# Attention and selective scan in one kernel: gates in the convolutions' banks, and new places for denominators, sums and statistics

## The chip, the core and the metric

The kernel runs on one core of a Trainium2 chip. The core has a matrix engine (TensorE, PE in the profile), a vector engine (VectorE, DVE), an activation engine (ScalarE, ACT), a general engine (GpSimd, POOL) and a sequencer that here only issues transfers (SyncE, SP). Each takes its instructions in the order in which the program issues them and waits on semaphores for the others. Matrix products are written to PSUM, which the kernel uses in banks of 128 partitions by 512 numbers. The metric is the device time in microseconds (us), the median over runs.

## The reference, cut to what matters

```python
x = x + attention(_gn(x), Wq, bq, Wkv, bkv)   # x: (8, 512, 48, 48); _gn: 32 groups of 16 channels
x = x + multiscale_mamba(_gn(x), ...)         # four blocks of 128 channels

# attention: 8 heads of 64, causal and linear, L = 2304 tokens
Q, K, V = elu(q) + 1, elu(k) + 1, v
den = 1 / (einsum('nhld,nhld->nhl', Q, cumsum(K)) + 1e-10)
S = S + k[..., :, None] * v[..., None, :];  o = einsum('nhk,nhkv->nhv', q, S)    # per token
out = o * den

# mamba, for block i of 4 (its input is block i plus the result of block i-1)
xp, z = split(u @ Wi.T)                       # 256 + 256 channels
xs = silu(causal_conv4(xp) + bc)
dt, Bm, Cm = split(xs @ Wx.T)                 # 8, 16, 16
delta = softplus(dt @ Wdt.T + bdt)
h = exp(delta * A) * h + (delta * xs) * Bm    # per token; 256 channels x 16 states
y = (sum_n(h * Cm) + xs * D) * silu(z)
xm = y @ Wo.T                                 # then fused with the input by a maximum and two sigmoids of means
```

Everything is float32.

## The kernel before, in words

The tokens of a sample are cut into six chunks of LC = 384. The Mamba part runs as 192 jobs, one for each sample, block of channels and chunk. Two streams take alternate samples, so that jobs of two samples interleave. A job consists of eight slots, a slot of four scans (`scan`, L830, 128x385 on DVE). Half slots are numbered through the whole program; a job has 16 of them, and this document counts them from 0 in each job.

For each scan ACT computes the factor exp(delta*A), called a decay (`decay`, L819), into a PSUM bank, and DVE reads it from there. In each slot DVE further computes one product for the next slot (`product`, L809), and POOL the last columns of that product (L798) and the weighting by C (L846). PE sums the weighted states (`gather`, L853) into `yp`. After four slots, half of the channels, `yp` is multiplied by the gate (`gated`, L865). When both halves are done, the output's projection (`project`, L871) and the maximum (L882) follow as a task called `finale`.

Six PSUM banks rotate. `take` hands out a free one, to decays and to all other work alike; a bank comes back at the place in the program where `free` is called, and whoever takes it next waits by semaphore until its last reader is done. `ahead(n)` issues decays as long as fewer than n are outstanding and a bank is free; n is 3 in the slots and 5 just before the two batches of activations named next.

Everything else is issued between the scans by tasks: generators that stop at a `yield` with a due time and the number of banks that they want. "1" means one half slot after the task's last step, a pair (h, gap) means at half slot h, and at least gap after the last step. `beside` is called in each half slot and steps the tasks that are due and whose banks are free. Each engine's order follows from this plan alone.

The tasks that matter here:

- `Job.prepare` prepares a job some ten slots before its first scan: the convolution as four products per half (`conv`, L635), the gates' products (`gate`, L646), a batch of four Silus on ACT (L670 to L675) with a load of the activation table before it and one after it, the projection to dt, B and C (L681, L686), the steps (L694) and a batch of two Softplus (L705), again between two table loads. In the steady state the Silu batch stands in half slot 14 and the Softplus batch in half slot 2 of the 16 that follow.
- `chunk` is the attention for one chunk, at half slots given by `times[m]`, usually half slot 3 of a job plus the number in `at(j)`: projections of q, k and v (L288), the feature map on ACT (L300, L301) and its end on DVE (L345, L353), the running sums of k (`kc`, L364), the product pr (L374), transposes of k and v (L381) and their copies kl and v (L385, L386), the denominators `den` and the state sums `ds` in one bank called `both` (L393, L398), the reciprocal and the additions to the state S (L401 to L410), the spread of the reciprocals over the rows (`rdb`, L414, and transposes `rb`, L418), and then scores and outputs (L423 to L454).
- `statistics` computes the group norm's statistics of a sample (`bn_stats`, L242, from pieces that `piece` loads, L248), `group_norm` the norm from them, and from those of the attention's result.
- `Stream.pass_on` moves a stream to its next block, and carries each chunk over with up to three activations (L596, L597, L601), which in the steady state stand in half slot 2.

Of the kernel before, what the change touches and what calls it, by code (L numbers as in the profile page):

```python
# [9 lines left out]
F32 = mybir.dt.float32  # L10
# [6 lines left out]
P = 128  # L17
# [32 lines left out]
def attention_then_mamba_kernel(  # L50
# [110 lines left out]

    def group_norm(stats, n, name, bufs):


        bank = Banks()
        yield "1", 1
        mv = small.tile([P, n, 2], F32, tag=f"mv{n}", name=f"mv_{name}", bufs=1)
        for ct in range(n):
            nc.vector.bn_aggr(mv[:, ct, :], stats[:, ct].rearrange("p c s -> p (c s)"))
        mean_ps = bank()  # L170
        nc.tensor.matmul(mean_ps[:, 0:n], grp, mv[:, :, 0], start=True, stop=True)
        yield "1", 0
        gm = small.tile([P, 3, n], F32, tag=f"gm{n}", name=f"gm_{name}", bufs=1)
        nc.vector.tensor_copy(gm[:, 0, :], mean_ps[:, 0:n])
        nc.vector.tensor_sub(gm[:, 1, :], mv[:, :, 0], mean_ps[:, 0:n])
        bank.free()
        if n == 1:
            nc.vector.tensor_scalar(
                gm[:, 2, :], gm[:, 1, :], gm[:, 1, :], mv[:, 0, 1:2], ALU.mult, ALU.add
            )  # L180
        else:
            nc.vector.tensor_mul(gm[:, 2, :], gm[:, 1, :], gm[:, 1, :])
            nc.vector.tensor_add(gm[:, 2, :], gm[:, 2, :], mv[:, :, 1])
        yield "0", 1
        var_ps = bank()
        nc.tensor.matmul(var_ps[:, 0:n], grp, gm[:, 2, :], start=True, stop=True)
        yield "1", 0
        nc.vector.tensor_scalar_add(gm[:, 2, :], var_ps[:, 0:n], 1e-5)
        bank.free()
        norm = small.tile([P, 3, n], F32, tag=f"norm{n}", name=f"norm_{name}", bufs=bufs)  # L190
        nc.gpsimd.tensor_tensor(norm[:, 0, :], gm[:, 2, :], power[:, 0:n], ALU.pow)
        yield "1", 0
        for i, factor in ((0, -1.0), (1, float(L))):
            for ct in range(n):
                nc.vector.tensor_scalar(
                    norm[:, 1 + i, ct : ct + 1],
                    gm[:, i, ct : ct + 1],
                    norm[:, 0, ct : ct + 1],
                    factor,
                    ALU.mult,  # L200
                    ALU.mult,
                )
        return norm
# [5 lines left out]
    def statistics(b):  # L209

        xv = x[b].rearrange("(t p) l -> p t l", p=P)
        stats = small.tile([P, 4, NC, 6], F32, tag="stats_a", name=f"stats_a{b}", bufs=1)
        if b == 0:
# [19 lines left out]
        else:  # L233
            for ct in range(4):
                for c in range(NC):
                    yield "2", 0
                    if (ct, c) == (0, 0):
                        nxt = piece(b, 0)
                    xs = nxt
                    i = ct * NC + c + 1  # L240
                    nxt = piece(b, i) if i < 4 * NC else None
                    nc.vector.bn_stats(stats[:, ct, c, :], xs)  # L242
        norms[b] = yield from group_norm(stats, 4, f"a{b}", 2)
# [24 lines left out]
    def chunk(m):  # L268
# [10 lines left out]
        def at(j, gap=1):  # L279
            return times[m] + j, gap  # L280
# [61 lines left out]
        ex = feature(qp, qb)  # L342
        yield at(2), 0
        q = new("q", 2)
        nc.vector.scalar_tensor_tensor(q, ex, 1.0, qp, ALU.min, ALU.add)  # L345
        bank.free()
        yield at(2, 0), 1
        kp, kb = project(1)
        yield at(3), 0
        ex = feature(kp, kb)  # L350
        yield at(4), 0
        k = new("k", 2)
        nc.vector.scalar_tensor_tensor(k, ex, 1.0, kp, ALU.min, ALU.add)  # L353
# [14 lines left out]
        if ksum is not None:  # L368
            kept = new("kept")
            nc.scalar.copy(kept[64:128], kc[64:128])  # L370
            save(ksum[:, cols], kept[64:128])
# [16 lines left out]

        yield at(12), 1
        both = bank()  # L390
# [5 lines left out]
        for i in range(more):  # L396
            for h in heads_of:
                nc.tensor.matmul(ds[h, i, :], kl[:, i, h], v[:, i, h], start=True, stop=True)  # L398
        yield at(14), 0
        rd = small.tile([P, 2 * NT], F32, tag="rd", name=f"rd_{n}", bufs=1)  # L400
# [5 lines left out]
        for i in range(more):  # L406
            if c == 0 and i == 0:
                nc.vector.tensor_copy(S[:, place[1], :], ds[:, 0, :])
            else:
                nc.vector.tensor_add(S[:, place[i + 1], :], S[:, place[i], :], ds[:, i, :])  # L410
        bank.free()
        yield at(15), 0
        rdb = new("rdb", 1, (P, 2 * NT, 64))
        nc.scalar.copy(rdb, rd.unsqueeze(2).to_broadcast([P, 2 * NT, 64]))  # L414
        yield at(16), 1
        rb = bank()[:, 0:LC].rearrange("p (i t) -> p i t", i=NT)
        for i in range(NT):
            nc.tensor.transpose(  # L418
                rb[:, i, :], rdb[:, 2 * i : 2 * i + 2, :].rearrange("p e d -> p (e d)"), ident
            )  # L420
        yield at(18), 0

# [33 lines left out]
        if c + 1 == NC:  # L456
            norm = yield from group_norm(stats, 1, f"m{b}_{o}", 8)
            flush()
            done[b, o] = norm
# [156 lines left out]
    class Job:  # L616
# [6 lines left out]
        def prepare(self):  # L623
# [19 lines left out]

            def gate(h):
                zp = bank()[:, 0:LC]
                nc.tensor.matmul(  # L646
                    zp,
                    wi[:, 256 + h * P : 256 + (h + 1) * P],
                    xi[:, c0 + 3 : c0 + 3 + LC],
                    start=True,  # L650
                    stop=True,
                )
                return zp

# [3 lines left out]
            converting.append(n)  # L658
            yield "1", 1
            xc0 = conv(0)  # L660
            yield "2", 2
            xc1 = conv(1)
            zp0 = gate(0)
            yield "1", 0
            xs = self.xs = mpool.tile([P, 2, LC], F32, tag="xs", name=f"xs_{n}")
# [4 lines left out]
            nc.scalar.activation(xs[:, 0, :], xc0, AF.Silu, bias=pv[:, 0:1])  # L670
            bank.free()
            zp1 = gate(1)
            nc.scalar.activation(xs[:, 1, :], xc1, AF.Silu, bias=pv[:, 1:2])
            nc.scalar.activation(sz[0], zp0, AF.Silu)
            nc.scalar.activation(sz[1], zp1, AF.Silu)  # L675
            converting.clear()
            bank.free(3, late=True)
            yield "1", 1
# [65 lines left out]
            for h in range(2):  # L744
                yield "1", 0
                nc.gpsimd.tensor_tensor(delta[:, h, :], delta[:, h, :], xs[:, h, :], ALU.mult)  # L746
            first = 2 * self.start
            yield "2", 0
# [208 lines left out]
    def finale(job):  # L957
        yield "0", 1
        job.project()
        yield "1", 0  # L960
        job.maximum()
        if job.c == NC - 1:
            yield from job.stream.pass_on()

    begun, put, counted = 0, 0, list(range(1, B))

    def begin(latest):

        nonlocal begun, put
        while counted and times[parts.index((counted[0], 0, 0))] - 64 <= half_no[0]:  # L970
            tasks.append(Task(statistics(counted.pop(0))))
# [52 lines left out]
    def at(k):  # L1024
        return jobs[k // SLOTS], k % SLOTS
# [166 lines left out]
```

## Time and profile before

| | |
|---|---|
| Median of 3 runs | 9329.64 us (9327.21 to 9330.81) |
| The profiled execution | 9323.3 us, of which 9321.5 us are the span from its first to its last instruction |
| Mean granted TensorE clock | 0.948 |
| First scan starts, last scan ends | 222.5 us, 9273.6 us |
| DVE idle between them | 785 us |
| Scans (L830) | 6144, mean 938 ns |
| Decays (L819) | 6144, mean 579 ns |
| Table loads on ACT | 768, 1283 ns each |

The profile shows one execution. A busy share counts an engine's instructions in the span; since neighbours overlap by some 0.08 us, this document also uses the time from the start of an instruction to the start of the next. A row of the wait view names who waited and for whom, then the total in us, the number of waits and the longest. A row of the timeline gives the start, the time it took, engine, line, operation, the tile written and those read, and the number of instructions that it merges; in brackets stands the idle time of the engine before it, and what ended it.

### The profile page before, as it was taken

The numbers are of one execution on the slowest core, as the hardware profiler recorded it, in microseconds if no ns is written. First come the engines' busy times: TensorE is split into PE (matmuls) and PEld (weight loads), VectorE is DVE, ScalarE is ACT, GpSimd is POOL, SyncE is SP. The second block draws the span as 40 slices with busy tenths as digits, with TensorE's granted clock in tenths as the row PEclk, the third lists the DMA queues.
The fourth block names the chain that finished last, engine by engine and source line by source line (L and its number), as shares of the span: only waits on it lengthen the run. The fifth ranks groups of instructions, "written<-read, shape, count | busy, mean of one in ns | idle before, by whom it ended". The sixth has DMA issues, their size and how long they took to land.

```text
span 9321.5 us, 120629 instructions
## 1 busy us (share of the span) xinstructions
PE 7735.1 (83%) x35714; PEld 3673.0 (39%) x35714; DVE 8348.4 (90%) x11640; ACT 6580.2 (71%) x12656; POOL 8080.8 (87%) x5635
## 2 busy tenths in 40 slices
PE   7888888888888888888888888888888888888865
PEld 4444444433344444443343444443333434444321
DVE  3899999999999999999999999999999999999997
ACT  3677777777777777777777777776777777777775
POOL 2788888889988898889998888888998888888998
PEclk9999999999999999999999999999999999999977
DMA  6566666667666666666766666667666666666654
GB/s 189 158 169 173 175 174 168 180 189 198 188 169 176 177 179 172 176 183 189 196 182 178 174 175 173 174 170 194 192 184 182 176 176 172 173 171 175 167 153 129
DMA packets 1002899, 1642.84 MB, mean 176 GB/s; under 512 B 138592, under 2 KB 797312, under 8 KB 1002240
## 3 DMA queue, kind: packets, MB, share of 16 engines
q1 hardware_dynamic: 1002240, 1635.13, 64.1%
q8 instruction: 283, 4.64, 0.2%
q14 instruction: 376, 3.08, 0.1%
HBM read 1309.06 MB, written 325.58 MB: 175 GB/s over the span
## 4 chain that ended last, share of the span: by engine, by line
DVE 39%; ACT 20%; PE 18%; issue 7%; DMA 7%; POOL 6%; SPq 2%; DVEq 0%; POOLq 0%; ACTq 0%
DVE u L830 23%; DVE u L809 8%; PE bank L288 7%; ACT bank L819 6%; PE bank L635 4%; POOL u L846 4%; ACT L819 3%; PE yp L853 3%; PE bank L646 2%; ACT L705 2%; DMA B<-scr 2%; DMA C<-scr 1%; ACT bank L301 1%; ACT delta L705 1%; DVE sm L436 1%
## 5 line engine op out<-in xcount | busy, mean ns | idle before, releaser
L830 DVE TENSOR_TENSOR_SCAN u<-bank,u 128x385 f32<-128x385 f32 (+1 forms) x6144 | 5475.1, 938 | 530.5 <-ACT bank L819 503.2
L846 POOL TENSOR_TENSOR u<-u,C 128x1536 f32<-128x1536 f32 x1536 | 4885.1, 3180 | 219.5 <-DVE u L830 112.6
L819 ACT ACTIVATE bank<-dr,av 128x385 f32<-128x385 f32 (+1 forms) x6144 | 3431.3, 579 | 1556.9 <-DVE u L830 1113.3
L853 PE MATMUL yp<-u,cst 128*64 128x384 f32 x12288 | 2429.9, 514 | 282.7 <-ACT yp L787 146.3
L798 POOL TENSOR_TENSOR u<-B,dxr 128x512 f32<-128x512 f32 x1536 | 1959.9, 1276 | 22.4 <-DMA dxr<-xscr 19.0
L288 PE MATMUL bank<-xn,wq_sb 128*128 128x384 f32 x4608 | 1855.1, 552 | 48.8 <-DVE u L830 31.7
L809 DVE TENSOR_TENSOR u<-B,dxp 128x1024 f32<-128x1024 f32 x1536 | 1834.7, 1195 | 10.7 <-ACT dxp L782 10.7
L853 PEld LDWEIGHTS yp<-u,cst 128*64 128x64 f32 x12288 | 788.3, 139 | 1476.6 <-issue 903.5
L635 PE MATMUL bank<-xi,wk 128*128 128x384 f32 x3072 | 1118.2, 507 | 280.1 <-ACT kl L385 172.7
L288 PEld LDWEIGHTS bank<-xn,wq_sb 128*128 128x128 f32 x4608 | 929.1, 212 | 862.9 <-issue 215.1
L635 PEld LDWEIGHTS bank<-xi,wk 128*128 128x128 f32 x3072 | 563.7, 193 | 862.2 <-ACT kl L385 254.1
L844 POOL COPY state<-u 128x4 f32<-128x4 f32 x1280 | 243.8, 190 | 740.6 <-DVE u L830 738.0
L300 ACT ACTIVATE ex<-bank,bqkv_sb 128x384 f32<-128x384 f32 x384 | 221.3, 576 | 561.6 <-PE bank L288 539.2
L787 ACT ACTIVATE yp<-xs,pv 128x384 f32<-128x384 f32 x384 | 223.4, 582 | 405.7 <-DVE yz L865 405.7
L819 ACT ACT_TABLE_LOAD x382 | 490.1, 1283 | 6.7
L746 POOL TENSOR_TENSOR delta<-delta,xs 128x384 f32<-128x384 f32 x384 | 385.8, 1005 | 95.5 <-DMA dscr<-delta 84.3
L418 PE MATMUL bank<-cst,rdb 128*128 128x128 f32 x576 | 112.7, 310 | 426.1 <-DVE u L830 334.7
L694 PE MATMUL bank<-dbc,wd 9*128 9x384 f32 x768 | 316.3, 524 | 65.1 <-ACT dbc L686 29.0
L646 PE MATMUL bank<-xi,wi 128*128 128x384 f32 x768 | 297.8, 500 | 59.8 <-ACT xs L670 59.8
L871 PE MATMUL bank<-yz,wo 128*128 128x384 f32 x768 | 297.6, 509 | 34.1 <-DVE yz L865 19.4
L449 PE MATMUL bank<-sm,v 128*64 128x128 f32 x2304 | 257.2, 301 | 42.4 <-DVE u L830 40.6
L418 PEld LDWEIGHTS bank<-cst,rdb 128*128 128x128 f32 x576 | 66.8, 153 | 558.9 <-ACT xb L601 272.5
(109 smaller groups left out, 7860.3 us busy)
## 6 DMA issues: line engine op xcount, KB each, us to landing
B<-scr SPq DMA_DIRECT2D x1536, 192.0 KB
C<-scr SPq DMA_DIRECT2D x1536, 192.0 KB
xn<-xn SPq DMA_DIRECT2D x192, 768.0 KB
dr<-dscr SPq DMA_DIRECT2D x768, 192.0 KB
dxr<-xscr SPq DMA_DIRECT2D x768, 192.0 KB
dscr<-delta SPq DMA_DIRECT2D x192, 384.0 KB
xscr<-delta SPq DMA_DIRECT2D x192, 384.0 KB
xn<-in_x SPq DMA_DIRECT2D x48, 768.0 KB
```

The costliest lines, as they stand in the source:

```text
L288: nc.tensor.matmul(ps, wq_sb[:, kt, j * 512 + o * P : j * 512 + (o + 1) * P], xn[:, kt, :], start=(kt == 0), stop=(kt == 3),)
L635: nc.tensor.matmul(xc, wk[:, k, h * P : (h + 1) * P], xi[:, c0 + k : c0 + k + LC], start=(k == 0), stop=(k == 3),)
L646: nc.tensor.matmul(zp, wi[:, 256 + h * P : 256 + (h + 1) * P], xi[:, c0 + 3 : c0 + 3 + LC], start=True, stop=True,)
L694: nc.tensor.matmul(vp, wd[32:41, h * P : (h + 1) * P], dbc[32:41, :], start=True, stop=True)
L746: nc.gpsimd.tensor_tensor(delta[:, h, :], delta[:, h, :], xs[:, h, :], ALU.mult)
L798: nc.gpsimd.tensor_tensor(u[:, :, :, 1 + LC - TAIL :], self.B[s % 4][:, :, cols].unsqueeze(2).to_broadcast(shape), self.dxr[s // 4][:, :, ...
L809: nc.vector.tensor_mul(u[:, :, :, 1 : 1 + LC - TAIL], self.B[s % 4][:, :, cols].unsqueeze(2).to_broadcast(shape), self.dxp.unsqueeze(1).to ...
L819: nc.scalar.activation(dA[:, cols], self.dr[h][:, g, cols], AF.Exp, scale=self.w[6][:, 2 * h + g, q + j : q + j + 1],)
L830: nc.vector.tensor_tensor_scan(u[:, j, g, cols], dA[:, cols], u[:, j, g, cols], 0.0, ALU.mult, ALU.add,)
L846: nc.gpsimd.tensor_tensor(h, h, self.C[s % 4].unsqueeze(2).to_broadcast([P, NG, 2, LC]), ALU.mult)
L853: nc.tensor.matmul(self.yp[g * 64 : g * 64 + 64, 0:LC], pair_sum, u[:, j, g, 1:], start=False, stop=(s % 4 == 3 and j == NG - 1), skip_gro ...
L871: nc.tensor.matmul(self.xm[:, 0:LC], self.w[2][:, h, :], self.yz[:, h, :], start=(h == 0), stop=(h == 1),)
```

## The change

The gates' products no longer take banks of their own: `gate(h, zp)` writes into the bank of the convolution once the Silu has read it. The steps of `prepare` up to there get fixed half slots. `den` and `ds` are computed two half slots earlier, and what follows from them as well; the transposes `rb` go into the bank `both` instead of a new one, so that it is held until q has been multiplied. The projection of k no longer comes after q's end, and q's end moves one half slot back. `kept` uses the buffer of `before`. The statistics of samples 2 to 7 are spread to one piece in 16 half slots, from two buffers, and the steps of `group_norm` get places of their own. `finale` asks for "1" instead of "0".

```diff
-    def group_norm(stats, n, name, bufs):
+    def group_norm(stats, n, name, bufs, places=("1", "1", "0", "1", "1")):
...
-            for ct in range(4):
-                for c in range(NC):
-                    yield "2", 0
-                    if (ct, c) == (0, 0):
-                        nxt = piece(b, 0)
-                    xs = nxt
-                    i = ct * NC + c + 1
-                    nxt = piece(b, i) if i < 4 * NC else None
-                    nc.vector.bn_stats(stats[:, ct, c, :], xs)
+            when = begins[b] + b % 2
+            for i in range(4 * NC):
+                yield (when - 2, 1) if b > 1 else "1", 0
+                xs = piece(b, i)
+                yield (when, 1) if b > 1 else "1", 0
+                nc.vector.bn_stats(stats[:, i // NC, i % NC, :], xs)
+                when += PERIOD
...
-        yield at(2), 0
-        q = new("q", 2)
+        yield at(2), 1
+        kp, kb = project(1)
+        yield at(3), 0
+        q, k = new("q", 2), new("k", 2)
         nc.vector.scalar_tensor_tensor(q, ex, 1.0, qp, ALU.min, ALU.add)
         bank.free()
-        yield at(2, 0), 1
-        kp, kb = project(1)
-        yield at(3), 0
         ex = feature(kp, kb)
         yield at(4), 0
-        k = new("k", 2)
...
-            kept = new("kept")
+            kept = new("before")
...
-        yield at(12), 1
+        yield at(10, 0), 1
         both = bank()
...
-        yield at(14), 0
+        yield at(12), 0
         rd = small.tile([P, 2 * NT], F32, tag="rd", name=f"rd_{n}", bufs=1)
...
-        bank.free()
-        yield at(15), 0
+        yield at(13), 0
         rdb = new("rdb", 1, (P, 2 * NT, 64))
         nc.scalar.copy(rdb, rd.unsqueeze(2).to_broadcast([P, 2 * NT, 64]))
-        yield at(16), 1
-        rb = bank()[:, 0:LC].rearrange("p (i t) -> p i t", i=NT)
+        yield at(14), 0
+
+        rb = both[:, 0:LC].rearrange("p (i t) -> p i t", i=NT)
...
-        yield at(18), 0
+        yield at(16), 0
 
         nc.vector.tensor_mul(q, q, rb.rearrange("p i t -> p (i t)"))
         bank.free()
...
-            norm = yield from group_norm(stats, 1, f"m{b}_{o}", 8)
+            norm = yield from group_norm(
+                stats, 1, f"m{b}_{o}", 8, [(times[m] + j, 1) for j in (28, 29, 29, 30, 31)]
+            )
...
-            def gate(h):
-                zp = bank()[:, 0:LC]
+            def gate(h, zp):
...
-            yield "1", 1
+            first = 2 * self.start
+            yield (first - 21, 0), 1
             xc0 = conv(0)
-            yield "2", 2
+            yield (first - 19, 2), 1
             xc1 = conv(1)
-            zp0 = gate(0)
-            yield "1", 0
+            yield (first - 18, 1), 0
...
             nc.scalar.activation(xs[:, 0, :], xc0, AF.Silu, bias=pv[:, 0:1])
-            bank.free()
-            zp1 = gate(1)
+
+            gate(0, xc0)
             nc.scalar.activation(xs[:, 1, :], xc1, AF.Silu, bias=pv[:, 1:2])
-            nc.scalar.activation(sz[0], zp0, AF.Silu)
-            nc.scalar.activation(sz[1], zp1, AF.Silu)
+            gate(1, xc1)
+            nc.scalar.activation(sz[0], xc0, AF.Silu)
+            nc.scalar.activation(sz[1], xc1, AF.Silu)
             converting.clear()
-            bank.free(3, late=True)
+            bank.free(2, late=True)
...
     def finale(job):
-        yield "0", 1
+        yield "1", 1
         job.project()
...
+    begins = {}
+    for b in counted:
+        first = times[parts.index((b, 0, 0))]
+        begins[b] = (first - 20) // PERIOD * PERIOD - 4 * NC * PERIOD - 2 if b > 1 else first - 64
...
-        while counted and times[parts.index((counted[0], 0, 0))] - 64 <= half_no[0]:
+        while counted and begins[counted[0]] - 4 <= half_no[0]:
             tasks.append(Task(statistics(counted.pop(0))))
```

## The prediction

> **What bounds the kernel now.** First the head of the page: VectorE (DVE) is the busiest engine.
>
> ```profile
> PE 7735.1 (83%) x35714; PEld 3673.0 (39%) x35714; DVE 8348.4 (90%) x11640; ACT 6580.2 (71%) x12656; POOL 8080.8 (87%) x5635
> ```
>
> The first scan starts at 222.5 us, the last ends at 9273.6; DVE is idle for 785 us between. Second, the waits of DVE in that stretch (who waited for whom: us in total, times, longest):
>
> ```profile
> DVE u L830 <- ACT bank L819: 503.2, 194, 4.7
> DVE q L345 <- ACT bank L301: 108.1, 54, 4.2
> DVE k L353 <- ACT bank L301: 56.6, 136, 1.0
> DVE gm_m L188 <- PE bank L186: 29.4, 31, 1.1
> ```
>
> A scan that waits for its decay is most of it: about once in each of the 192 jobs. Third, the timeline of one job's end on DVE, ACT and PE (start, us, engine, line):
>
> ```profile
> 4247.63 1.19 DVE L809 TENSOR_TENSOR u<-B,dxp 128x1024 f32<-128x1024 f32 x1
> 4248.74 2.65 DVE L830 TENSOR_TENSOR_SCAN u<-bank,u 128x385 f32<-128x385 f32 x3
> 4254.33 0.96 DVE L830 TENSOR_TENSOR_SCAN u<-bank,u 128x385 f32<-128x385 f32 x1 [2.94 <-ACT bank L819]
> ```
>
> ```profile
> 4247.91 1.10 ACT L819 ACTIVATE bank<-dr,av 128x385 f32<-128x385 f32 x2
> 4249.03 1.28 ACT L670 ACT_TABLE_LOAD   x1
> ...
> 4251.91 0.49 ACT L675 ACTIVATE sz<-bank 128x384 f32<-128x384 f32 x1
> 4252.42 1.28 ACT L819 ACT_TABLE_LOAD   x1
> 4253.71 1.09 ACT L819 ACTIVATE bank<-dr,av 128x385 f32<-128x385 f32 x2
> ```
>
> ```profile
> 4247.69 2.85 PE L635 MATMUL bank<-xi,wk 128*128 128x384 f32 x8 [1.29 <-ACT kl L385]
> 4250.38 1.49 PE L646 MATMUL bank<-xi,wi 128*128 128x384 f32 x4
> ```
>
> ACT leaves the decays for a batch of four Silus between two table loads. Three decays are ready; DVE uses them up and waits 2.94 us. The softplus batch has the same shape, and four decays ready:
>
> ```profile
> 4260.39 1.20 DVE L809 TENSOR_TENSOR u<-B,dxp 128x1024 f32<-128x1024 f32 x1
> 4261.50 3.50 DVE L830 TENSOR_TENSOR_SCAN u<-bank,u 128x385 f32<-128x385 f32 x4
> 4264.92 1.20 DVE L809 TENSOR_TENSOR u<-B,dxp 128x1024 f32<-128x1024 f32 x1
> 4266.03 0.55 DVE L865 TENSOR_TENSOR yz<-yp,sz 128x384 f32<-128x384 f32 x1
> 4266.94 1.81 DVE L830 TENSOR_TENSOR_SCAN u<-bank,u 128x385 f32<-128x385 f32 x2 [0.36 <-issue]
> ```
>
> ```profile
> 4262.78 1.28 ACT L705 ACT_TABLE_LOAD   x1
> 4264.08 0.87 ACT L705 ACTIVATE delta<-bank 128x384 f32<-128x384 f32 x2
> 4264.97 1.28 ACT L819 ACT_TABLE_LOAD   x1
> 4266.26 0.59 ACT L819 ACTIVATE bank<-dr,av 128x385 f32<-128x385 f32 x1
> ```
>
> Four scans, the product and yz just last until the next decay ends at 4266.85: no wait for ACT, and nothing to spare.
>
> **What the Trainium skill says.** "ScalarE: Activation LUTs", What ACT_TABLE_LOAD costs: about 1283 ns for the load plus about 1380 ns of drain. The load agrees (1283 ns in the rows); the drain does not show: the next activation starts 1.29 us after the load's start, and I use that. "PSUM — Partial Sum Buffer", Engine vs sequencer instructions: ACT's queue is strictly first in, first out, and matmuls run in program order. The trace agrees (the gates L646 start as the convolution's eight L635 end), so a static order decides what can hide. "Perfetto Trace Analysis", Identifying the Most-Contended Engine: a bubble that repeats can mean too few buffers. Here it is one per job, and the buffers are the six PSUM banks.
>
> **The change, part by part.** I use durations from start to start of neighbours, as the timelines give them: scan 0.86, product L809 1.11, other 384-wide DVE operations 0.45 to 0.47, decay 0.52, table load 1.29. A job is 8 slots, 16 half slots. All counts come from the order in which both programs' instructions stand on each engine.
>
> (1) Silu batch, ACT's side. Gates now write the banks of the two convolutions, so each waits for its Silu; and den and ds (L393, L398), moved two half slots up, now stand on PE between the second convolution and the gates, in 173 of 190 jobs. Their own runs took 0.83 and 0.57 us, 1.40 together. Before, gate 0 starts 1.35 us after the table load's start and sz at 2.24; after, gate 0 at 2.75, gate 1 0.64 later, its end (0.85 on) at 4.25, the last Silu at 4.28 instead of 2.88. The next decay is 1.40 us later. Were PE not delayed, the wait for the Silus alone would cost about 0.6 (xs ends at 1.87, a gate takes 0.80); that is the low end, 1.8 the high one if den waits for more.
>
> (2) Silu batch, DVE's side. Decays ready: before 6 banks less xc0, xc1 and zp0 are 3; after, 6 less xc0, xc1 and `both` are 3. The bank saved by the gates goes to den. But rd, its reciprocal and the three S additions (L401 to L410), before two half slots later, now stand ahead of the awaited scan: 0.17+0.11+3x0.20=0.88 us (the 4258 us stretch of the timeline shows them). The spread bn_stats (L242, 0.46) fall there too: 144 in 190 windows against 18, 0.31 a job; bn_aggr and smaller ones about 0.1. Cover rises from 4.61 to 5.90. Sum: before, the wait is 495 us at the scan plus 29 at L188 in the same window, 524 (2.76 a job). After: +1.40-1.29=+0.11 a job, x190=+21: 545 us.
>
> (3) Softplus batch. The denominators' transposes (rb) now reuse `both`, which is held from half slot 13 until q is multiplied in half slot 3 of the next job. At softplus (half slot 2) two banks hold its inputs and one is `both`: 3 decays ready in 173 jobs, where 4 were in all of them. From the start s of the scan that frees the last bank, DVE has scan 0.86, product 1.11, three scans 2.57, q L423 0.45: 4.99 us. ACT: the scan's end at 0.94+0.03, decay 0.52, then in 110 jobs L596, L597, L601 (0.52+0.51+0.60; in the order before they stood ahead of that decay, now behind it), and 4.09 to the end of the next decay (the last fence: 4262.78 to 4266.85), plus 0.03. That is 7.23, a wait of 2.24 us; 1.64 in 30 jobs without L601, 0.62 in 34 without all three: 246+49+21=316 us. Before it was nothing. This is the largest term. Its low end is 230 (ACT finds part of L596 to L601 done earlier), its high end 340.
>
> (4) k's projection (L288) is issued without waiting for q, and q (L345) is computed half a slot later. q's operands are then ready long before; k gains q's 0.47 us and fg's place as cover, against a mean wait of 0.41. With L418's bank wait gone (335 us on PE in the wait view, ahead of L288), I take both waits as gone: -165. Low end of the gain 60, if k's projection is late instead.
>
> (5) Statistics: one load and one bn_stats per 16 half slots instead of every two; norms are ready before their chunk. SP no longer stands 87 us behind bn_stats, which nobody on DVE pays for; norm_a's wait for POOL (12 us) goes: -12. The x loads and the xr load, moved up past C and B loads on SP, are 0.3 to 0.5 us of issue each and wait for nothing late; kept now shares a buffer with `before`, which kc's matmul has read by then and whose store is issued ten half slots before the next load. The m norms move to half slots 15 to 2, inside the two stalls: nothing.
>
> (6) The output's projection: its yield changes from "0" to "1", but the task is created before the half number is advanced, so one half has already passed. PE's order has it at the same place (behind q's L288, ahead of the next gathers). Nothing; if it did move, PE would gain at most its 34 us of waiting, off DVE's path.
>
> Sum against the profiled execution (9323.3 us, span 9321.5): +21+316-165-12=+160, 9483. The runs' median lies 6 above it (9329.6): 9490 us.
>
> **The rivals.**
> Faster: in a tenth of the jobs before, the second convolution starts 4.4 us before the table load and not 1.3. If den and ds run that early, the gates are not delayed: -1.40x190=-266, 9224 us. It decides once 160/190=0.85 of the 1.40 us hide. Against it: 179 convolutions wait for ACT's kl copy in the new order, 121 before. A fourth ready decay in the Silu window would do the same, were `both` not held there.
> Slower still: 100 of the 165 us of q and k waits stay, because ACT enters their half slots 2 us later: 9590 us. It begins to count when the second relu ends over 1 us later than now. For it: L300 waited 463 us for PE. Against it: ACT catches up within a slot or two, since a slot is 4.5 us of DVE and 2.2 of decays.
> No change: the fill of rd, S and bn_stats (1.29 a job, 245 us) and q, k balance the batches; it needs the softplus wait halved: 9330. The order gives no reason.
>
> **How the numbers follow.** My forecast has a chance of 0.72, slower still 0.14, faster 0.10, no change 0.04. Low end: the softplus and the gate term both halfway to their low ends, (316-230)/2=43 and (1.40-0.6)x190/2=76, give 9371, taken as 9375. High end: the q and k gain at its low end, +105, gives 9595, taken as 9600; the slower rival (9590) lies inside, the faster and no change (0.14 together) outside. A measurement tells about 0.2% (19 us) from no change: faster 0.10, same 0.04, slower 0.86.
>
> **What would show it.** In the new profile: a wait of scans for ACT at softplus, some 170 times, near 2 us (step 3; its absence fells the forecast); in the Silu window ACT idle before its third and fourth Silu, some 1.4 us (1), with PE's den between convolution and gates; rd ahead of the awaited scan (2); q and k waits near zero (4); the projection in its old place (6). DVE's busy time should stay near 8348. Were it to change by over 50 us, the sum over waits would be the wrong account.

## The result, and the profile after

The changed kernel takes 9656.94 us (median of 4 runs, 9653.41 to 9660.79), the kernel before 9328.49 us in the same series. The ratio is 1.0352, with a 95% interval from 1.0334 to 1.037: the change costs 3.5%. The forecast was 9490 us, at most 9600. The sign was right, the size was not. One run of the kernel before with `rb` in `both`, told below, took 23227 us at a granted clock of 0.316; it is left out of that kernel's median, and every other run below lies within 0.4% of the median of its kernel.

The profiled execution took 9660.8 us, with a span of 9659.0 us and a mean granted TensorE clock of 0.927 (0.948 before). Most lines move up by 2 to 4: the scan is now L826, the decay L815, the feature map L298 and L299, q and k L345 and L349, the projections L286 and L867, the maximum L878, the gather L849. The head of the page:

```profile
PE 7992.6 (83%) x35714; PEld 3749.9 (39%) x35714; DVE 8388.6 (87%) x11640; ACT 6630.6 (69%) x12656; POOL 8082.6 (84%) x5635
```

The instruction counts are the same as before. DVE's busy time is 40 us longer; the rest of the 337 us between the two spans is idle time of DVE, which grew by 293 us between the first and the last scan (785 to 1078) and by 4 us outside. The waits of DVE in that stretch, as before (who waited for whom: us in total, times, longest):

```profile
DVE u L826 <- ACT bank L815: 640.4, 335, 3.5
DVE rd L397 <- PE bank L394: 192.3, 182, 4.2
DVE k L349 <- ACT bank L299: 89.0, 77, 2.0
DVE fg L878 <- PE bank L867: 49.8, 32, 2.2
```

The scans wait 335 times where it was 194. Placed on the half slots of a job, this is one wait of 327 us in all at the Silu batch (176 times), and a second one of 307 us at the softplus batch (154 times) that the kernel before doesn't have. `rd`, the maximum `fg` and k are further waits; q waits no longer. In this stretch of the kernel before, `rd` waited once (0.9 us) and `fg` not at all.

One Silu batch of the changed kernel, on DVE, ACT and PE (start, us, engine, line; in brackets the idle time before and what ended it):

```profile
4358.64 0.17 DVE L397 TENSOR_SCALAR rd<-bank 128x6 f32<-128x6 f32 x1 [1.11 <-PE bank L394]
...
4360.02 0.94 DVE L826 TENSOR_TENSOR_SCAN u<-bank,u 128x385 f32<-128x385 f32 x1
4362.54 0.96 DVE L826 TENSOR_TENSOR_SCAN u<-bank,u 128x385 f32<-128x385 f32 x1 [1.58 <-ACT bank L815]
```

```profile
4357.80 0.57 ACT L669 ACTIVATE xs<-bank,pv 128x384 f32<-128x384 f32 x1
4359.48 0.49 ACT L671 ACTIVATE sz<-bank 128x384 f32<-128x384 f32 x1 [1.10 <-PE bank L643]
4360.12 0.49 ACT L672 ACTIVATE sz<-bank 128x384 f32<-128x384 f32 x1 [0.15 <-PE bank L643]
4360.63 1.28 ACT L815 ACT_TABLE_LOAD   x1
```

```profile
4357.37 0.72 PE L389 MATMUL bank<-cst,pr 128*128 128x2 f32 x6
4358.03 0.57 PE L394 MATMUL bank<-v,kl 128*64 128x64 f32 x12
4358.53 1.56 PE L643 MATMUL bank<-xi,wi 128*128 128x384 f32 x4
```

On PE the denominators and the state sums (L389, L394) stand ahead of the gates (L643), so ACT idles before its third and fourth Silu. `rd` itself waits on DVE for L394, 1.11 us here. One stall has become two shorter ones around `rd` and the three additions to S.

A softplus batch of the same job, DVE and ACT:

```profile
4371.23 0.95 DVE L826 TENSOR_TENSOR_SCAN u<-bank,u 128x385 f32<-128x385 f32 x1
4374.41 0.96 DVE L826 TENSOR_TENSOR_SCAN u<-bank,u 128x385 f32<-128x385 f32 x1 [2.23 <-ACT bank L815]
```

```profile
4370.31 1.28 ACT L702 ACT_TABLE_LOAD   x1
...
4373.79 1.09 ACT L815 ACTIVATE bank<-dr,av 128x385 f32<-128x385 f32 x2
```

The scan at 4371.23 uses the last decay that was ready; ACT enters its table loads at 4370.31 and comes back with a decay at 4374.4. DVE stands for 2.23 us.

### The profile page after: what moved, and what is told of

It is laid out like the page before. It is cut to its first block, busy times and chain, and to the rows that moved or that the text cites. A ratio compares the mean times of both kernels' runs of the same rounds, so it can differ in the third digit from the quotient of the medians.

```text
span 9659.0 us, 120018 instructions
## 1 busy us (share of the span) xinstructions
PE 7992.6 (83%) x35714; PEld 3749.9 (39%) x35714; DVE 8388.6 (87%) x11640; ACT 6630.6 (69%) x12656; POOL 8082.6 (84%) x5635
## 4 chain that ended last, share of the span: by engine, by line
DVE 33%; ACT 22%; PE 20%; POOL 9%; issue 9%; DMA 6%; SPq 2%; DVEq 0%; POOLq 0%; ACTq 0%
DVE u L826 19%; ACT bank L815 7%; DVE u L805 7%; PE bank L633 6%; POOL u L842 5%; ACT L815 4%; PE bank L286 4%; PE yp L849 3%; PE bank L643 3%; DMA C<-scr 2%; ACT L702 2%; POOL u L794 2%; ACT delta L702 1%; DVE yz L861 1%; PE bank L867 1%
## 5 line engine op out<-in xcount | busy, mean ns | idle before, releaser
L826 DVE TENSOR_TENSOR_SCAN u<-bank,u 128x385 f32<-128x385 f32 (+1 forms) x6144 | 5497.7, 939 | 671.4 <-ACT bank L815 640.4
L815 ACT ACTIVATE bank<-dr,av 128x385 f32<-128x385 f32 (+1 forms) x6144 | 3433.7, 579 | 1562.7 <-DVE u L826 1339.1
L849 PE MATMUL yp<-u,cst 128*64 128x384 f32 x12288 | 2676.7, 546 | 160.5 <-POOL u L842 126.2
L286 PE MATMUL bank<-xn,wq_sb 128*128 128x384 f32 x4608 | 1801.5, 537 | 136.2 <-DVE u L826 108.8
L849 PEld LDWEIGHTS yp<-u,cst 128*64 128x64 f32 x12288 | 854.6, 146 | 1497.9 <-issue 961.6
L286 PEld LDWEIGHTS bank<-xn,wq_sb 128*128 128x128 f32 x4608 | 910.0, 209 | 1100.1 <-DVE u L826 375.9
L867 PE MATMUL bank<-yz,wo 128*128 128x384 f32 x768 | 374.9, 581 | 380.4 <-DVE yz L861 368.6
L298 ACT ACTIVATE ex<-bank,bqkv_sb 128x384 f32<-128x384 f32 x384 | 220.2, 573 | 631.7 <-PE bank L286 631.7
L691 PE MATMUL bank<-dbc,wd 9*128 9x384 f32 x768 | 339.3, 553 | 103.7 <-DVE u L826 70.2
L867 PEld LDWEIGHTS bank<-yz,wo 128*128 128x128 f32 x768 | 145.7, 210 | 547.5 <-DVE yz L861 466.7
L643 PE MATMUL bank<-xi,wi 128*128 128x384 f32 x768 | 304.1, 516 | 19.6 <-ACT xs L666 19.4
L377 PE MATMUL bank<-cst,vT 128*128 128x128 f32 x576 | 102.9, 288 | 226.0 <-DVE pr L370 214.8
```

Of the source, the lines that this page charges most:

```text
L286: nc.tensor.matmul(ps, wq_sb[:, kt, j * 512 + o * P : j * 512 + (o + 1) * P], xn[:, kt, :], start=(kt == 0), stop=(kt == 3),)
L643: nc.tensor.matmul(zp, wi[:, 256 + h * P : 256 + (h + 1) * P], xi[:, c0 + 3 : c0 + 3 + LC], start=True, stop=True,)
L691: nc.tensor.matmul(vp, wd[32:41, h * P : (h + 1) * P], dbc[32:41, :], start=True, stop=True)
L815: nc.scalar.activation(dA[:, cols], self.dr[h][:, g, cols], AF.Exp, scale=self.w[6][:, 2 * h + g, q + j : q + j + 1],)
L826: nc.vector.tensor_tensor_scan(u[:, j, g, cols], dA[:, cols], u[:, j, g, cols], 0.0, ALU.mult, ALU.add,)
L849: nc.tensor.matmul(self.yp[g * 64 : g * 64 + 64, 0:LC], pair_sum, u[:, j, g, 1:], start=False, stop=(s % 4 == 3 and j == NG - 1), skip_gro ...
```

## The experiments

All kernels here compute the whole output; only places, orders and banks differ. Each series has its own runs of the kernel before (9321 to 9331 us), and ratios are to these.

### Which edit costs the time: `rb` in the denominators' bank

The first theory is step 3 of the prediction: what costs is the bank that `both` holds through the softplus batch. Two runs test it from both sides. The first takes the changed kernel, frees `both` after S, and gives the transposes their own bank two half slots later, as before:

```diff
+        bank.free()
         yield at(13), 0
...
-        yield at(14), 0
-        rb = both[:, 0:LC].rearrange("p (i t) -> p i t", i=NT)
+        yield at(16), 1
+        rb = bank()[:, 0:LC].rearrange("p (i t) -> p i t", i=NT)
...
-        yield at(16), 0
+        yield at(18), 0
         nc.vector.tensor_mul(q, q, rb.rearrange("p i t -> p (i t)"))
```

> The kernel after, with the transposes rb back in a bank of their own, taken two half slots later (as before the change), and `both` freed after the additions to S. Softplus has four decays ready again. Theory A (the bank held through the softplus batch makes DVE late, and q's, k's and the maximum's waits follow from that): the 307 us of scan waits at softplus fall to under 20, the 369 us that PE stands at the projection for yz to under 100, the k and maximum waits (138 us) to under 50; time 9657-307-100 = about 9250. Theory B (PE stands at the projection whatever the softplus batch does, since it is free earlier): only the 307 go, PE still waits over 250 us for yz, k and maximum waits stay over 100; time about 9350.

Measured: 9320.43 us, ratio 0.9998 (0.9989 to 1.0006). Its wait view for DVE has left of the scans' waits

```profile
DVE u L826 <- ACT bank L815: 348.6, 187, 3.6
```

and these stand at the Silu batch. The scans' waits at softplus are gone, and with them the whole loss of 336 us. The time is nearer to theory B, but the lateness on PE went as theory A has it: the output's projection waits 33 us for yz instead of 369, and k and `fg` together wait 66 us instead of 139. This run also moves the transposes and q's multiplication back by two half slots. The second run moves nothing; it puts `rb` into `both`, alone, in the kernel before:

```diff
-        bank.free()
         yield at(15), 0
...
-        yield at(16), 1
-        rb = bank()[:, 0:LC].rearrange("p (i t) -> p i t", i=NT)
+        yield at(16), 0
+        rb = both[:, 0:LC].rearrange("p (i t) -> p i t", i=NT)
```

> The kernel before, with rb put into `both` and nothing else changed. Theory A: the same held bank alone takes a decay from the softplus batch (three ready in 176 of 183 batches, four before): a new scan wait there near 2 us where the carry's three activations fall behind the last decay, some 250 us in all, and the k wait (57 us) grows; time 9328+250 to 350 = 9580 to 9680. Theory B: without the other edits q waits are as they were; 9328+250 = about 9580 and no more.

Measured: 9641.97 us (median of three runs), ratio 1.0342 (1.0324 to 1.0359). Its line for the scans is

```profile
DVE u L829 <- ACT bank L818: 914.6, 374, 4.7
```

against 503.2 and 194 times. 391 us of the new wait stand in half slot 3, behind softplus, and q's wait falls from 108 to 37 us, probably because it comes behind that new stall. As theory A has it, the held bank alone makes the kernel before 3.4% slower, and taking it out of the changed kernel gives all of the loss back. Everything else in the change adds up to nothing that can be measured (0.9998 in the first run).

Since the bank is short at softplus, the batch could also come later, when q has freed it:

```diff
             spreading.append(n)
-            yield "1", 0
+            yield "2", 0
             delta = mpool.tile([P, 2, LC], F32, tag="delta", name=f"delta_{n}", bufs=1)
```

> The kernel after, rb still in `both`, with the Softplus batch one half slot later, when q has been multiplied and `both` is free: four decays are ready again in 177 of 183 batches, and the carry's activations stand ahead of them. Theory A (only the missing bank at the batch costs): scan waits there fall from 307 us to under 30, as with rb in its own bank; about 9657-335 = 9320. Theory B (rb in `both` costs by the place of its transposes too, or a later batch delays q's and k's activations): at most half of it returns, 9480 or more.

Measured: 9956.66 us, ratio 1.0679 (1.0663 to 1.0695). The scans' waits at softplus are gone (DVE is idle for 9 us in half slot 3), but q's projection now takes the bank that the softplus's input frees. In PE's wait view:

```profile
PE bank L286 <- ACT delta L702: 681.1, 146, 5.2
```

The maximum, whose projection stands behind it on PE, makes DVE wait for 687 us. Theory A fell: four decays at the batch did not bring the time back, since the shortage of banks was only moved, and got dearer.

### Step 4: what became of the q and k waits

The prediction took 165 us off for q and k. The new order of q and k, alone in the kernel before:

```diff
-        yield at(2), 0
-        q = new("q", 2)
+        yield at(2), 1
+        kp, kb = project(1)
+        yield at(3), 0
+        q, k = new("q", 2), new("k", 2)
         nc.vector.scalar_tensor_tensor(q, ex, 1.0, qp, ALU.min, ALU.add)
         bank.free()
-        yield at(2, 0), 1
-        kp, kb = project(1)
-        yield at(3), 0
         ex = feature(kp, kb)
         yield at(4), 0
-        k = new("k", 2)
```

> The kernel before with the new order of q and k alone. Theory A (the forecast's step 4): the waits for q (108 us) and k (57 us) both go, -165: about 9155. Theory B (PE takes k's projection only behind the gather that waits for ACT's skip of yp, and the maximum's product stands close to it): q's waits go, k's stay at 40 to 120 us, some 30 to 50 us of waits for the maximum's product are new, so the gain is 20 to 70: about 9275.

Measured: 9326.53 us, ratio 1.0001 (0.9993 to 1.001). DVE's waits:

```profile
DVE fg L880 <- PE bank L869: 109.8, 54, 4.5
DVE k L351 <- ACT bank L301: 36.3, 108, 2.2
```

q's 108.1 us in 54 jobs are gone, and `fg`, which did not wait, now waits 109.8 us in 54 jobs, 42 of them the same. Theory B had this exchange, but with less than half the size. PE's timeline in one such job:

```profile
4206.48 0.72 PE L416 MATMUL bank<-cst,rdb 128*128 128x128 f32 x3 [2.79 <-DVE u L828]
4207.23 4.24 PE L288 MATMUL bank<-xn,wq_sb 128*128 128x384 f32 x8
4211.31 1.45 PE L869 MATMUL bank<-yz,wo 128*128 128x384 f32 x4
```

PE stands 2.79 us for the bank of the transposes (L416), then runs q's projection, then the output's projection. q's end needs the first of these two, the maximum the second; q's old place on DVE took the wait, and once q is out of the way the maximum takes it. The wait belongs to PE's lateness, not to q's place. In 27 of the jobs, which make 90 of the 110 us, the bank that PE stands for is released by the softplus batch. k's wait falls by 20 us only.

The row of L288 shows a second thing: eight matmuls take 4.24 us, where the same eight take 2.85 in most places. In the kernel before, q's projection takes over 3.3 us in 130 of the 181 chunks after the first scan, and with it go nearly all of q's waits. This is taken up below.

For k the next suspect was PE's order: the gather (L853 before) waits there until ACT has set `yp`, and k's projection stands behind it. The timeline of PE in the kernel with denominators and m norms put back (told below; L865 is the output's projection, L847 the gather, L286 k's projection):

```profile
4321.55 1.51 PE L865 MATMUL bank<-yz,wo 128*128 128x384 f32 x4
4324.96 1.51 PE L847 MATMUL yp<-u,cst 128*64 128x384 f32 x8 [1.90 <-ACT yp L781]
4326.40 2.85 PE L286 MATMUL bank<-xn,wq_sb 128*128 128x384 f32 x8
```

A first attempt asked for k's projection one half slot earlier in that kernel:

```diff
-        yield at(2), 1
+        yield at(1, 0), 1
         kp, kb = project(1)
```

> As the kernel with the m norms free, and k's projection issued one half slot earlier, ahead of the gather that waits for ACT's skip. Theory: k waits because PE has its projection behind that gather; its 114 us fall below 30, some 80 to 100 us less than without this edit. Rival: the wait is handed on, since one bank more is held for half a slot: scans or the maximum wait instead, and the time is the same within 30 us or longer.

Measured: 9223.0 us, ratio 0.9886 (0.9871 to 0.99), against 9227.53 without it, and k waits 126 us as before. The edit does not move what it meant to move: after the first 302 us PE's order is the same in both kernels. This run says nothing on the theory. The next moves the gather instead, behind the tasks of half slot 5:

```diff
-                if len(waiting) > 1:
+                if len(waiting) > 1 and s != 2:
                     waiting.pop(0)()
...
                 beside(2 * k + 1)
+                if s == 2 and len(waiting) > 1:
+                    waiting.pop(0)()
```

> The kernel with the denominators in their old places and the m norms free, and in each job's half slot 5 the gather issued behind the tasks instead of ahead of them: PE's order becomes q's projection, the output's projection, k's projection, gather. Theory: k waits for ACT's relu because its projection stands behind the gather, which stands 1.9 us until ACT has set yp; k's 126 us fall below 30 and the time to some 9130 us. Rival: the gather comes 2.9 us later, and what waits for it or for the step's tile takes the time back: 9210 us or more.

Measured: 9101.45 us, ratio 0.9754 (0.9737 to 0.9771), 126 us below the kernel without it. k's waits fall from 126.3 us to 2.8, DVE's idle time by 109 us. PE's own wait for `yp` is the visible difference: without the edit the wait view of PE begins with

```profile
PE yp L847 <- ACT yp L781: 284.8, 174, 3.9
```

and with it this line is no longer among the longest. So k waited because its projection was queued behind a gather that waits for ACT. The same edit in the changed kernel as it is:

> The kernel of after with one edit: in each job's half slot 5 the gather is issued behind the tasks instead of ahead of them, so that k's projection stands ahead of it on PE. Theory: the 88 us of k's wait that are left in after are this order's, and the softplus wait (307 us) is not touched: k below 15 us, the time some 9575 us. Rival: behind the late softplus batch k's relu is late by ACT's own queue: k keeps 60 us or more, 9630 to 9660 us.

Measured: 9592.54 us, ratio 1.0281 (1.0264 to 1.0298), 64 us below the changed kernel. k falls from 89.0 to 44.8 us, `fg` from 49.8 to 30.9; the softplus wait stays (306). Half of k's wait was this order's. Of the 63 waits that are left, 62 come after PE has stood at the output's projection for yz, which DVE computes late behind the softplus stall, with k's projection next in PE's order. The run with `rb` in its own bank agrees (k waits 35 us there), but no run takes this part out alone.

### The other edits, one at a time

Gates in the convolutions' banks, alone in the kernel before (`gate(h, zp)`, two banks instead of three, as in the diff of the change):

```diff
-            zp0 = gate(0)
...
-            zp1 = gate(1)
+            gate(0, xc0)
...
+            gate(1, xc1)
```

> The kernel before with the gates in the convolutions' banks alone. The denominators do not take the bank that this frees, so the Silu batch has four decays ready, not three. Theory A (the bank saved and the wait of the gates for their Silus nearly balance): one decay and its scan more is -0.86 us, the gates' wait is +0.6 with PE free, so -0.2 to -0.3 us a job: about 9275. Theory B (the gates' wait costs as much as after the change, 1.1 us, even without den and ds ahead of them): about 9365.

Measured: 9339.26 us, ratio 1.0016 (1.0008 to 1.0023). With the fourth ready decay DVE's idle time at the Silu batch (half slots 14, 15 and 0) falls from 531 us to 408, but k waits 134 us (57 before) and `rd` 68 us (1 before), which use it up. The result lies between the two theories. The profiled execution was the slowest of the 20, at 9361 us.

Statistics and norms in their new places, alone in the kernel before (the edits to `statistics`, `group_norm`, its call and `kept`):

```diff
-            norm = yield from group_norm(stats, 1, f"m{b}_{o}", 8)
+            norm = yield from group_norm(
+                stats, 1, f"m{b}_{o}", 8, [(times[m] + j, 1) for j in (28, 29, 29, 30, 31)]
+            )
```

> The kernel before with the statistics' and norms' new places alone (and kept in before's buffer, without which the second statistics buffer does not fit). Theory A: the spread bn_stats fall into the Silu window (0.3 us a job, -60), norm_a's 12 us go, and the last step of the m norms now waits for POOL's power (+40): about 9300. Theory B: the fixed places cost more than they fill: 9330 to 9350.

Measured: 9338.08 us, ratio 1.0012 (1.0005 to 1.0019). Theory B holds. DVE's idle time in half slot 15 falls from 451 to 429 us, but that is `gm_m` L188, whose 29 us of waits go from there; the scans at the Silu batch wait 8 us longer (503 instead of 495), although 144 `bn_stats` stand in half slots 14 and 15 where 18 stood. And `norm_m` waits for POOL 30 times, 36.8 us in all; it waited once before, 0.7 us.

The output's projection truly half a slot later, in the changed kernel:

```diff
     def finale(job):
-        yield "1", 1
+        yield "2", 1
         job.project()
```

> The kernel after, with the output's projection one half slot later in fact (its task asks for two half slots). Theory A: the projection is not the cause, but it passes the delay on to k: PE's 369 us of waiting for yz go under 50, the k and maximum waits (138 us) under 60, the softplus waits (307 us) stay; time about 9657-100 = 9560. Theory B: the same, with up to 140 us gained, 9520. If the k wait stays at 88 us, its cause is neither, and the time stays within 30 us of 9657.

Measured: 10038.25 us, ratio 1.0765 (1.0749 to 1.0781). Both theories fell, and not only in size: they forecast a gain, and it lost 381 us. Scans now wait at half slot 5 too (154 us), k waits 232 us and `fg` 149, and ACT waits 910 us for the projections L286. Whether the bank that the projection takes or its place in PE's order does this was not taken apart.

### Putting the denominators back, and a faster version

The changed kernel with the denominators, sums and `rb` all in their old places:

```diff
-        yield at(10, 0), 1
+        yield at(12), 1
         both = bank()
...
-        yield at(12), 0
+        yield at(14), 0
         rd = small.tile([P, 2 * NT], F32, tag="rd", name=f"rd_{n}", bufs=1)
...
+        bank.free()
+        yield at(15), 0
...
+        yield at(16), 1
+        rb = bank()[:, 0:LC].rearrange("p (i t) -> p i t", i=NT)
```

> The kernel after, with the denominators wholly as before the change (den, ds, rd, rdb, rb in their old half slots and banks); gates, q and k, statistics as in the change. Both batches have four decays ready. Theory A: scan waits at softplus under 20 us; at the Silus one decay more (0.86) and the gates behind their Silus (+0.6), so about 1.7 us a job, 320 us against 524; q and k waits near zero; time about 9328-200-165 = 8965. Theory B: the k and maximum waits stay (138 us), since PE stands for yz at the projection: about 9100.

Measured: 9240.05 us, ratio 0.9907 (0.9885 to 0.993): below the kernel before, though above the forecasts of both theories. Four decays are ready at both batches. DVE's idle time at Silu is 424 us in half slots 14, 15 and 0, of which 345 are the scans'. `fg` waits 9 us and q not at all; k waits 114 us. Gates, q and k, and statistics each gained nothing alone, and together they gain 0.9%. With `rb` in its own bank the early denominators cost 80 us (9320 against 9240).

With the m norms' places as before as well (the lines after this call move up by 2):

```diff
-            norm = yield from group_norm(
-                stats, 1, f"m{b}_{o}", 8, [(times[m] + j, 1) for j in (28, 29, 29, 30, 31)]
-            )
+            norm = yield from group_norm(stats, 1, f"m{b}_{o}", 8)
```

> The kernel of after with the denominators in their old places, and the norms of the attention's result (m) without fixed places again. Theory: the fixed places cost the 37 us of norm_m for POOL and the 73 us of gm_m L174 seen with the denominators moved back; both go, about 9240 - 100 = 9140 us. Rival: these waits stand inside the Silu batch's stall, the scan then waits instead: at most 30 us go, 9210 to 9240 us.

Measured: 9227.53 us, ratio 0.989 (0.9874 to 0.9907), 12 us less, which is not clear of the spread of either (9216 to 9259 and 9216 to 9242). The rival holds: `norm_m` falls from 37 to 14 us and the 73 us of `gm_m` L174 go, and the scans at Silu (371 instead of 333 us in half slot 0), `gm_m` L188 (22) and `rd` (20) wait in their place. This is the kernel in which moving the gather then gives 9101.45 us, 2.5% below the kernel before and the fastest of all that ran.

## Why the prediction was wrong

The forecast's sum was +160 us; the profiled executions differ by 337. The terms, by the half slots in which DVE is idle:

| Step | forecast | measured | |
|---|---|---|---|
| (1), (2) Silu batch | +21 | +43 | half slots 14, 15 and 0: 531 to 574 us |
| (3) softplus batch | +316 | +330 | half slot 3: 0 to 330 us |
| (4) q and k, with `fg` | -165 | -25 | half slots 5 and 7: 175 to 150 us |
| (5) norms, and the rest | -12 | -28 | all other half slots but 4 |
| half slot 4 | none | -27 | 31 to 4 us |
| DVE's busy time | 0 | +40 | 8348.4 to 8388.6 us |
| outside the scans | 0 | +4 | 149 to 153 us |

- **Step 3 was right, in mechanism and size.** The median wait in half slot 3 is 2.23 us; the prediction worked out 2.24. The run that takes the edit out and the one that adds it alone both show the held bank to be as large as the whole slowdown. The remark on repeating bubbles that the prediction takes from the Trainium skill stands in "Perfetto Trace Analysis", Optimization Strategy; these two runs agree with it, by 336 and 321 us.
- **Step 4 is the one that failed.** It read "I take both waits as gone: -165", with a low end of 60 us; the measured gain is 25. q's wait did go, and so did PE's stand for the transposes' bank. But k's wait grew from 57 to 89 us, and `fg`, which the step counts only as cover for k, took on 50. The step did not ask what else PE has to wait for ahead of k's projection and of the output's. k's projection still stood behind the gather, which is half of k's wait, and behind the output's projection, which waits for yz. `fg` was late for another reason than in the run with this edit alone: in 29 of its 32 waits, 48 of the 50 us, the m norm's matmul (L186), which step 5 moves, had stood on PE for the bank that the softplus batch releases, and the gather, q's and the output's projection came right behind it. The waits of PE in the changed kernel:

```profile
PE bank L867 <- DVE yz L861: 368.6, 156, 4.7
PE bank L186 <- ACT delta L702: 91.4, 29, 3.2
```

  In the kernel before, the first of these was 19 us and the second was none. With `rb` in its own bank L186 has no such wait, and `fg` waits 32 us in 45 jobs, only one of them among these 32; no run tests the link from L186 to `fg` alone. This step makes 140 of the 177 us that the forecast was short.
- **The remaining 37 us** are what is left of misses of both signs (the other rows of the table), so that the smaller terms came close in sum partly by luck.
- **Steps 1 and 2 had the mechanism, with a size off by 22 us.** ACT idles 1.32 us inside the batch (0.27 before), and from the start of the last decay ahead of it to the end of the first behind it are 7.10 us instead of 5.97, so +1.13 where 1.40 was forecast. But `rd` does not fill the stall for nothing: it waits for L394 itself, 183 us in 176 jobs. And the `bn_stats` that the step counts as a fill did not shorten the scans' waits in the run with the statistics alone.
- **Step 5**: norm_a's wait fell by half (12 us to 5.5) where all of it was to go. "The m norms ... nothing" does not hold: alone in the kernel before they cost 37 us of waiting for POOL. In the changed kernel, whose scans wait at softplus just before, that is 1.2 us, but there the norms' matmul makes PE late for `fg`.
- **Step 6 was right** that the yield "1" leaves the projection where it was; the run with "2" shows what a true move does.
- **Busy time**: "should stay near 8348" missed by 40 us, within the 50 that was allowed. 723 waits of over 60 ns instead of 522 account for part of it: neighbours overlap by some 0.08 us, and 201 more waits lose some 16 us. Longer instructions make the other 20 or so; why is open.
- **The rivals**: "slower still" (9590, 100 of the 165 us stay) came nearest; 140 stayed. It gave ACT's late entry as its cause; in the trace ACT itself stands for PE's projections ahead of nearly all of k's waits (88 of 89 us).

## What to carry to other kernels

When buffers rotate in a pool that feeds the bound engine, count for each batch that interrupts the feed how many are ready; one bank held across it cost 3.4%, and the bank saved elsewhere did not pay for it. Before a wait is booked as gain, follow it to the engine that is late, and list everything that this engine waits for and everything queued behind it: here whoever stood next took the wait over. If a producer's queue holds an instruction that waits for a third engine, moving it behind the urgent work (here the gather, 126 us) can be worth more than moving the consumer.

## What was not expected of the hardware

PE runs the same matmuls at two speeds within one execution. Eight 128x384 matmuls of a projection take 2.85 us in most places; in the row of L288 above, behind a wait, 4.24. The trace records the clock that was granted to TensorE, as full speed (1.0) or half (0.5), and it agrees: the mean over that row is 0.66, over the output's projection right behind it 1.00. In the kernel before, 134 of the 576 projections take over 3.3 us. The clock is at half speed in part of 128 of them, and in part of 1 of the 442 others.

The Trainium skill describes this in "TensorE: Matmul & The Clock Gate", Part 1: The HAM clock gate: PE's clock is halved after an idle window of about 3.4 us and comes back after as much sustained work. The traces agree on the two speeds, but PE need not stand still for that long. Between the first and the last scan of the kernel before there are 201 stretches at half speed; in the 3.41 us ahead of them PE was busy for 36% in the median, and an idle stretch of 3.4 us or more reached into only 15 of these. Of 159 projections with an idle stretch of 2 us or more ending in the 6 us ahead, 114 took over 3.3 us, and of 194 with none above 0.3 us, 2 did. The length of one stretch does not decide it, though: with a longest stretch of 0.3 to 1 us none of 144 were slow in the kernel before, but 51 of 120 in the changed kernel.

So a wait of PE for a bank can cost more than its length. The slow projections go along with the waits of q and `fg`: of 181 projections of q, 130 took over 3.3 us in the kernel before, 117 with q and k moved alone, and 11 with the denominators put back, where `fg` waits 9 us and the mean clock is 0.970. That the slow clock is the cause of those waits was not tested alone.
